# A four-layer graph network, last layer: each block's own columns on VectorE instead of through a diagonal matrix, and block 0's columns taken from on-chip memory

## The chip, the cores and the metric

The kernel runs on one core of one Trainium2 chip. The metric is the device time of one launch, in microseconds (us). The times before are three runs: 1054.39, 1056.62 and 1062.56 us, median 1056.62 us.

## The reference, cut to what matters

Four graph layers act on `x` (2708 nodes, 512 features) with a sparse weighted adjacency `adj` (2708 x 2708, every diagonal element non-zero). The change touches the last one only:

```python
bw  = sign(L3_gnn_weight)                  # 512 x 512
xw  = maximum(sign(x), 0) @ bw.T           # whole numbers, 2708 x 512
x   = layernorm(x + relu(adj @ xw))        # the last layer, and the output
```

`xw` holds whole numbers of at most 512 in size, so float16 holds them exactly. `adj` is float32.

## The kernel before, in words

The 2708 nodes are cut into 22 blocks of 128 rows (the last, block 21, has 20). Node 0 has the most neighbours and the density falls with the node's number, so the kernel treats the blocks in two ways:

- **Whole blocks**, 0 to 4 (`WHOLE3 = 5`): the product with all 2708 columns is formed densely, in 22 steps `j`, one for each block of source nodes. `whole_tile(j)` loads 128 rows of `xw` as float16 (`xs`), widens them to the 4-byte matmul type (`widened`), loads 128 x 640 elements of the transposed adjacency (`aw`), splits them into a high and a low half (`halves_of`: ScalarE copies the rounded value, VectorE subtracts it from the original), and runs 5 blocks x 2 halves = 10 matmuls of 128x128 by 128x512 (line L2001).
- **Sparse blocks**, 21 and then 5 to 20 (`order3`): for each block the nodes that any of its rows needs were listed earlier, in tiles of 128. `packed[b]` holds the matching columns of the adjacency, and GpSimd gathers the rows of `xw` by an indirect DMA per tile (`gathered`, line L584, tile `xg`; 76 gathers in this layer). Each tile costs two matmuls (L2040), one for each half. Blocks whose nodes nearly all are neighbours of block 0 take block 0's rows straight from `xw0`, which is on chip (`direct(b)`). GpSimd is used for the gathers alone in this layer.

A sparse block's own nodes are not in its list. Their only element is the diagonal `dia_own[:, b]`. Before, that product was a matmul too: the block's own `xw` rows are loaded (`xo`, L2013, two buffers) and widened (`wo`), ScalarE (L2021) and VectorE (L2024) build the high and the low half of a 128x128 diagonal matrix `dp`, and two matmuls (L2029) open the block's sum.

`finish3` closes a block: VectorE adds `relu(sum)` to the old features from PSUM (L1952), takes the statistics (L1954, L1956) and a few small steps for the inverse root, in pairs of blocks. ScalarE scales the row (L1969) and SyncE writes it out (L1973). The last block, 20, goes through this alone.

Two things set the order of the work. The loop over `order3` runs whole tiles between sparse blocks, a whole tile for each three gathers issued (`FETCHES3`), so that TensorE has work while gathers arrive. The tile scheduler then fixes a static order of instructions on each engine; every engine runs its own list in order. Buffers that matter: `parts` (high and low halves) has 4, `wide` (widened rows) 4, `aw` 4, `xs` 4, `xo` 2, gathered rows `xg` 11, PSUM sums of sparse blocks 3.

`packed[0]`, the transposed adjacency's columns of block 0 for all 22 source blocks, has been on chip since the first layer, but the whole blocks load these columns again as the first 128 of the 640.

Of the kernel before, what the change touches and what calls it, by code (L numbers as in the profile page):

```python
# [8 lines left out]
F32 = mybir.dt.float32  # L9
F32R = mybir.dt.float32r  # L10
# [3 lines left out]
AF = mybir.ActivationFunctionType  # L14
ALU = mybir.AluOpType
# [4 lines left out]
P = 128  # L20
# [27 lines left out]
WHOLE3 = 5  # L48
# [447 lines left out]
def sparse_layers(ctx, tc, x, adj, adj_t, w0_t, b0, w_sa, a_sa, w_gcnb, b_gcnb, wa, ba, wb, bb, w3_t,  # L496
# [11 lines left out]
    nc = tc.nc  # L508
    N, D = x.shape
    KC = D // P  # L510
    NB = -(-N // P)
# [1405 lines left out]
    with tc.tile_pool(name="s_l3", bufs=11, reuse_waits="tile") as lp, \  # L1917
# [1 line left out]
            tc.tile_pool(name="s_ps_3", bufs=3, reuse_waits="tile", space=PSUM) as ps_3:  # L1919
        W3 = WHOLE3 * P  # L1920
        CH3 = 4
        PW = max(CH3 * P, W3)

        def halves_of(a, r: int, w: int, name: str):

            p = lp.tile([P, 2, PW], F32R, tag="parts", name=f"p{name}", bufs=4)
            low, high = p[:r, 0, :w], p[:r, 1, :w]
            nc.scalar.copy(high, a)
            nc.vector.tensor_tensor(low, a, high.bitcast(F32), op=ALU.subtract)
            return p  # L1930
# [2 lines left out]

        def widened(t, r: int, name: str):

            g = lp.tile([P, D], F32R, tag="wide", name=f"w{name}", bufs=4)
            turn[0] += 1
            if turn[0] % 3 == 0:
                nc.vector.tensor_copy(g[:r], t[:r])
            else:  # L1940
                nc.scalar.copy(g[:r], t[:r])
            return g

        moments = []

        def finish3(b: int, ps, more: bool):

            m = rows(b)
            old = f[b] if b else first[1]
            k = len(moments)  # L1950
            t = old[:, :D]
            nc.vector.scalar_tensor_tensor(t[:m], ps[:m], 0.0, t[:m], op0=ALU.max, op1=ALU.add)  # L1952
            st = small.tile([P, 6], F32, tag="st", name=f"st_3_{b}")
            nc.vector.bn_stats(st[:m], t[:m])  # L1954
# [30 lines left out]

        whole = [ps_w.tile([P, D], F32, tag=f"w{b}", name=f"l3_{b}") for b in range(WHOLE3)]

        def whole_tile(j: int):
# [21 lines left out]
        for at, b in enumerate(order3):  # L2010
            m = rows(b)
            xo = lp.tile([P, D], F16, tag="xo", name=f"xo{b}", bufs=2)
            nc.sync.dma_start(xo[:m], xw_rows[b * P : b * P + m, :])  # L2013
            xo = widened(xo, m, f"o{b}")
            if at + 1 < len(order3) and at:
                gather3(order3[at + 1])
            src = [xw0] * len(direct(b)) + sources3.pop(b)
            ps = ps_3.tile([P, D], F32, tag="mm", name=f"l3_{b}")

            dp = lp.tile([P, 2, P], F32R, tag="dp", name=f"dp{b}", bufs=2)  # L2020
            nc.scalar.activation(  # L2021
                dp[:m, 1, :m], ident[:m, :m], AF.Copy, scale=dia_own[:m, b : b + 1]
            )
            nc.vector.scalar_tensor_tensor(  # L2024
                dp[:m, 0, :m], ident[:m, :m], dia_own[:m, b : b + 1],
                dp[:m, 1, :m].bitcast(F32), op0=ALU.mult, op1=ALU.subtract,
            )
            for h in range(2):
                nc.tensor.matmul(  # L2029
                    ps[:m], dp[:m, h, :m], xo[:m, :], start=(h == 0), stop=False  # L2030
                )
            for i0 in range(0, tiles(b), CH3):
                n = min(CH3, tiles(b) - i0)
                p = halves_of(
                    packed[b][:, i0 : i0 + n, :].rearrange("p n i -> p (n i)"), P, n * m,
                    f"{b}_{i0}",
                )
                for i in range(n):
                    for h in range(2):
                        nc.tensor.matmul(  # L2040
                            ps[:m], p[:, h, i * m : (i + 1) * m], src[i0 + i],
                            start=False, stop=(i0 + i == len(src) - 1 and h == 1),
                        )
# [88 lines left out]
```

## Time and profile before

| | |
|---|---|
| runs | 1054.39, 1056.62, 1062.56 us |
| profiled execution | 1000.5 us |
| its span, first to last instruction | 998.8 us |
| TensorE clock granted, mean | 0.968 |
| busy over the span | TensorE 88%, VectorE 66%, GpSimd 55%, ScalarE 39% |
| last layer: first product to last instruction | 881.0 to 998.8 us |

The page of the profile gives busy time by engine, the span in 40 slices, the DMA queues, the chain of work that ended last, and the costliest groups of instructions. A line such as "L1952 DVE SCALAR_TENSOR_TENSOR f<-l,f ... x21 | 14.4, 685 | 4.9 <-PE l L2040 4.8" says: line 1952, on VectorE, writes `f` from `l` and `f`, 21 times, 14.4 us busy, 685 ns each on average, 4.9 us idle of the engine just before these, 4.8 of it ended by a TensorE matmul of line 2040. PE is TensorE, PEld its weight loads, DVE VectorE, ACT ScalarE, POOL GpSimd, SP SyncE. Durations of instructions that run back to back overlap a little at their ends, so the spacing of their starts is the better price in a full queue. The profiled execution is 56 us shorter than the median of the runs; no view shows where the difference lies.

### The profile page before, as it was taken

What the parts mean: (1) busy time and instruction counts of PE and PEld (TensorE: products, weight loads), DVE (VectorE), ACT (ScalarE), POOL (GpSimd) and SP (SyncE); (2) the same over time, 40 slices, a digit from 0 to 9 for tenths busy, and PEclk for the clock granted to TensorE, in tenths of its full rate; (3) what the DMA queues carried; (4) which work ended last, traced back from release to release, by engine and by line L of the source; (5) the groups of instructions that cost most, each with busy time, mean ns of one, the idle gap of its engine ahead of it and who ended that gap; (6) DMA issues with size and microseconds to landing.
All of it is one profiled execution on the core that took longest, in us unless ns stands there. A gap on an engine that the chain in (4) does not pass through costs nothing.

```text
span 998.8 us, 13107 instructions
## 1 busy us (share of the span) xinstructions
PE 875.6 (88%) x3775; PEld 458.8 (46%) x3793; DVE 657.8 (66%) x2571; ACT 386.5 (39%) x821; POOL 549.6 (55%) x580
## 2 busy tenths in 40 slices
PE   1899997198999889999999989988989999789993
PEld 1555553022233244555555533444545555458872
DVE  4889998235677745555554356666768777647776
ACT  3667672000000125544444333333334333246564
POOL 1688888777777367645332154434343333057773
PEclk9999999599999999999999999999999999979998
DMA  9999984477778577766544476768487566289997
GB/s 275 351 360 363 359 273 118 131 217 230 243 248 256 157 223 217 225 186 207 190 138 126 138 265 242 249 225 273 156 264 231 191 200 209 86 248 340 356 262 230
DMA packets 96294, 231.16 MB, mean 231 GB/s; under 512 B 14204, under 2 KB 27884, under 8 KB 96212
## 3 DMA queue, kind: packets, MB, share of 16 engines
q0 software_dynamic: 46896, 139.22, 46.3%
q1 hardware_dynamic: 37368, 76.25, 22.2%
q10 hardware_dynamic: 11948, 14.76, 4.6%
q8 instruction: 32, 0.52, 0.2%
q14 instruction: 50, 0.41, 0.1%
HBM read 188.51 MB, written 31.71 MB: 220 GB/s over the span
## 4 chain that ended last, share of the span: by engine, by line
PE 53%; DMA 20%; DVE 16%; issue 4%; ACT 3%; POOL 3%; ACTq 0%; POOLq 0%; DVEq 0%; SPq 0%
PE l L1318 11%; DMA xg<-x_rows,i 10%; PE h L1535 8%; DMA xg<-y_rows,i 7%; PE l L2001 5%; PE a L1746 4%; PE e L1746 4%; PE l L2040 3%; PE y L1047 3%; PE pg L1798 2%; DVE s_mask L828 2%; PE pc L1798 2%; PE e L1568 2%; PE a L1569 2%; POOL xg L584 1%
## 5 line engine op out<-in xcount | busy, mean ns | idle before, releaser
L1723 POOL DMA_INDIRECT xg<-x_rows,i x107 | 105.3, 984 | 170.3 <-PE a L1746 39.9
L584 POOL DMA_INDIRECT xg<-x_rows,i x107 | 103.7, 969 | 95.8 <-PE l L1318 60.7
L1014 POOL DMA_INDIRECT a<-in_adj_t_dram,row_at x107 | 115.9, 1083 | 52.2 <-issue 24.9
L584 POOL DMA_INDIRECT xg<-y_rows,i x107 | 105.9, 989 | 32.6 <-issue 13.1
L1318 PE MATMUL l<-xg,a 128*64 128x512 f32 (+1 forms) x214 | 99.8, 628 | 27.2 <-DMA xg<-y_rows,i 26.5
L584 POOL DMA_INDIRECT xg<-xw_rows,i x76 | 79.0, 1039 | 31.2 <-issue 12.9
L1746 PE MATMUL a<-xg,a 128*64 128x512 f32 (+1 forms) x214 | 92.8, 603 | 3.3 <-DMA xg<-x_rows,i 3.3
L1746 PE MATMUL e<-xg,ae 128*64 128x512 f32 (+1 forms) x214 | 90.3, 603 | 3.1 <-ACT ae L1496 2.9
L1047 PE MATMUL y<-s_w,xt 128*128 128x512 f32 (+1 forms) x176 | 83.6, 620 | 0.0
L1535 PE MATMUL h<-s_wsa,xt 128*128 128x256 f32 (+3 forms) x352 | 82.0, 386 | 0.1
L1318 PE MATMUL l<-xg,inc 128*64 128x512 f32 (+1 forms) x214 | 78.0, 604 | 3.0 <-DMA xg<-x_rows,i 3.0
L1535 PEld LDWEIGHTS h<-s_wsa,xt 128*128 128x128 f32 (+1 forms) x352 | 63.9, 186 | 25.7 <-ACT xt L1530 9.9
L1491 ACT ACTIVATE ae<-sl,xg 128x64 f32<-128x64 f32 (+1 forms) x107 | 37.6, 360 | 98.4 <-DMA xg<-x_rows,i 90.4
L1318 PEld LDWEIGHTS l<-xg,a 128*64 128x64 f32 (+1 forms) x214 | 24.6, 153 | 81.3 <-DMA xg<-y_rows,i 61.0
L765 ACT ACTIVATE unused<-arow 128x1408 uint8<-128x1408 f32 (+3 forms) x44 | 58.4, 1326 | 3.2 <-DMA x_rows<-s_zero 2.4
L1426 DVE SCALAR_TENSOR_TENSOR t<-l,s_dinv,f 128x512 f32<-128x512 f32 (+1 forms) x21 | 15.7, 749 | 55.6 <-PE l L1318 55.6
L613 ACT ACTIVATE rsqs<-mv 128x1 f32<-128x1 f32 (+2 forms) x56 | 11.3, 202 | 100.3 <-DVE mv L642 95.6
L2001 PE MATMUL l<-ws,pw 128*128 128x512 f32 (+1 forms) x210 | 50.1, 392 | 0.0
L1492 DVE SCALAR_TENSOR_TENSOR ae<-ae 128x128 f32<-128x128 f32 (+5 forms) x56 | 19.3, 344 | 45.1 <-ACT ae L1491 44.8
L1047 PEld LDWEIGHTS y<-s_w,xt 128*128 128x128 f32 (+1 forms) x176 | 32.5, 195 | 34.5 <-issue 34.4
L1798 PE MATMUL pg<-s_wg,pt 128*128 128x256 f32 (+1 forms) x176 | 44.6, 391 | 3.0 <-ACT pt L1786 3.0
L638 DVE BATCH_NORM_STATS2 st<-t 128x6 f32<-128x512 f32 (+1 forms) x66 | 45.2, 685 | 0.2
(302 smaller groups left out, 1813.6 us busy)
## 6 DMA issues: line engine op xcount, KB each, us to landing
arow<-in_adj_dram SPq DMA_DIRECT2D x21, 704.0 KB
arow<-in_adj_dram SPq DMA_DIRECT2D x21, 650.0 KB
x_rows<-f SPq DMA_DIRECT2D x41, 256.0 KB
aw<-in_adj_t_dram SPq DMA_DIRECT2D x21, 320.0 KB
f<-in_x_dram SPq DMA_DIRECT2D x20, 256.0 KB
y_rows<-yt ACTq DMA_DIRECT2D x20, 256.0 KB
out_dram<-f SPq DMA_DIRECT2D x20, 256.0 KB
x_rows<-h SPq DMA_DIRECT2D x19, 257.0 KB
```

Of the source, the lines that this page charges most:

```text
L584: nc.gpsimd.indirect_dma_start(out=t, out_offset=None, in_=src[:, :], in_offset=bass.IndirectOffsetOnAxis(ap=index[b][:, i : i + 1], axis=0),)
L638: nc.vector.bn_stats(st[:m], t[:m])
L765: nc.scalar.activation(unused[:m, : ar.shape[1]], ar, AF.Copy, accum_out=row_sums[:m, b, h : h + 1])
L1014: nc.gpsimd.indirect_dma_start(out=packed[b][:, t + len(direct(b)), :], out_offset=None, in_=adj_t, in_offset=bass.IndirectOffsetOnAxis(ap ...
L1047: nc.tensor.matmul(ps[:m], xt[:, k, :m], w0[:, k, :], start=(k == 0), stop=(k == KC - 1))
L1318: nc.tensor.matmul(ps[r0:r1], weights, moving, start=(i == order[0]), stop=all(span(b, j) != (r0, r1) for j in order[order.index(i) + 1 :] ...
L1491: nc.scalar.activation(ev[:, i, :], sl, AF.Identity, bias=score)
L1535: nc.tensor.matmul(ps, xt[:, k, :m], w[:, k, :], start=(k == 0), stop=(k == KC - 1))
L1723: nc.gpsimd.indirect_dma_start(out=g, out_offset=None, in_=x2_rows[:, :], in_offset=bass.IndirectOffsetOnAxis(ap=index[b][:, t : t + 1], a ...
L1746: nc.tensor.matmul(ps[r0:r1], weights, moving, start=(i == order[0]), stop=all(span(b, k) != (r0, r1) for k in order[order.index(i) + 1 :] ...
L1798: nc.tensor.matmul(ps, pt[:, k, :m], w[:, k, :], start=(k == 0), stop=(k == KC - 1))
L2001: nc.tensor.matmul(whole[b], p[:r, h, b * P : (b + 1) * P], g[:r, :], start=(j == 0 and h == 0), stop=(j == NB - 1 and h == 1),)
```

## The change

1. Sparse blocks: the diagonal matrix, its two matmuls and the widening of the own rows go. `finish3` gets the float16 row `xo` and starts with one VectorE instruction, `u = xo * dia_own + sum` (float16 row from SBUF, sum from PSUM, float32 result in SBUF, one buffer). The relu-and-add then reads `u` instead of PSUM.
2. Whole blocks: `aw` is loaded without its first 128 columns (128 x 512 instead of 128 x 640), and block 0's weights come from `packed[0]`, split into halves for four steps `j` at a time (`parts0`, two buffers).
3. `wide` has 3 buffers instead of 4 and now serves the whole tiles only, so every third of these is widened on VectorE. `halves_of` takes its shape as (tiles, width).

```diff
-        PW = max(CH3 * P, W3)
-        def halves_of(a, r: int, w: int, name: str):
-            p = lp.tile([P, 2, PW], F32R, tag="parts", name=f"p{name}", bufs=4)
-            low, high = p[:r, 0, :w], p[:r, 1, :w]
+        PW = max(CH3 * P, W3 - P)
+        def halves_of(a, r: int, shape, name: str, tag: str = "parts", bufs: int = 4):
+            n, w = shape
+            p = lp.tile(
+                [P, 2, PW if tag == "parts" else CH3 * P], F32R, tag=tag, name=f"p{name}", bufs=bufs
+            )
+            p = p[:, :, : n * w].rearrange("p h (n i) -> p h n i", n=n)
+            low, high = p[:r, 0], p[:r, 1]
             nc.scalar.copy(high, a)
             nc.vector.tensor_tensor(low, a, high.bitcast(F32), op=ALU.subtract)
...
-            g = lp.tile([P, D], F32R, tag="wide", name=f"w{name}", bufs=4)
+            g = lp.tile([P, D], F32R, tag="wide", name=f"w{name}", bufs=3)
...
-        def finish3(b: int, ps, more: bool):
+        def finish3(b: int, ps, more: bool, own=None):
...
+            if own is not None:
+                u = lp.tile([P, D], F32, tag="u3", name=f"u3_{b}", bufs=1)
+                nc.vector.scalar_tensor_tensor(
+                    u[:m], own[:m], dia_own[:m, b : b + 1], ps[:m], op0=ALU.mult, op1=ALU.add
+                )
+                ps = u
             nc.vector.scalar_tensor_tensor(t[:m], ps[:m], 0.0, t[:m], op0=ALU.max, op1=ALU.add)
...
-            a = lp.tile([P, W3], F32, tag="aw", name=f"aw{j}", bufs=4)
-            nc.sync.dma_start(a[:r], adj_t[j * P : j * P + r, :W3])
-            p = halves_of(a[:r], r, W3, f"w{j}")
+            a = lp.tile([P, W3 - P], F32, tag="aw", name=f"aw{j}", bufs=4)
+            nc.sync.dma_start(a[:r], adj_t[j * P : j * P + r, P:W3])
+            p = halves_of(
+                a[:r].rearrange("p (n i) -> p n i", n=WHOLE3 - 1), r, (WHOLE3 - 1, P), f"w{j}"
+            )
+            if j % CH3 == 0 or j == NB - 1:
+                n = min(CH3, NB - 1 - j) if j < NB - 1 else 1
+                first_block[:] = j, halves_of(
+                    packed[0][:r, j : j + n, :], r, (n, P), f"z{j}", "parts0", 2
+                )
+            j0, p0 = first_block
             for b in range(WHOLE3):
                 for h in range(2):
+                    weights = p[:r, h, b - 1, :] if b else p0[:r, h, j - j0, :]
                     nc.tensor.matmul(
-                        whole[b], p[:r, h, b * P : (b + 1) * P], g[:r, :],
+                        whole[b], weights, g[:r, :],
...
             nc.sync.dma_start(xo[:m], xw_rows[b * P : b * P + m, :])
-            xo = widened(xo, m, f"o{b}")
...
-            dp = lp.tile([P, 2, P], F32R, tag="dp", name=f"dp{b}", bufs=2)
-            nc.scalar.activation(
-                dp[:m, 1, :m], ident[:m, :m], AF.Copy, scale=dia_own[:m, b : b + 1]
-            )
-            nc.vector.scalar_tensor_tensor(
-                dp[:m, 0, :m], ident[:m, :m], dia_own[:m, b : b + 1],
-                dp[:m, 1, :m].bitcast(F32), op0=ALU.mult, op1=ALU.subtract,
-            )
-            for h in range(2):
-                nc.tensor.matmul(
-                    ps[:m], dp[:m, h, :m], xo[:m, :], start=(h == 0), stop=False
-                )
...
-                            start=False, stop=(i0 + i == len(src) - 1 and h == 1),
+                            start=(i0 + i == 0 and h == 0),
+                            stop=(i0 + i == len(src) - 1 and h == 1),
...
-            finish3(b, ps, not pending and b not in (order3[0], order3[-1]))
+            finish3(b, ps, not pending and b not in (order3[0], order3[-1]), xo)
```

More of the change, by code (lines that the diff above doesn't have):

```diff
@@ L1986, in sparse_layers @@
         whole = [ps_w.tile([P, D], F32, tag=f"w{b}", name=f"l3_{b}") for b in range(WHOLE3)]
+        first_block = [0, None]
         def whole_tile(j: int):
@@ L2018, in sparse_layers @@
             ps = ps_3.tile([P, D], F32, tag="mm", name=f"l3_{b}")
-            dp = lp.tile([P, 2, P], F32R, tag="dp", name=f"dp{b}", bufs=2)
-            nc.scalar.activation(
-                dp[:m, 1, :m], ident[:m, :m], AF.Copy, scale=dia_own[:m, b : b + 1]
-            )
-            nc.vector.scalar_tensor_tensor(
-                dp[:m, 0, :m], ident[:m, :m], dia_own[:m, b : b + 1],
-                dp[:m, 1, :m].bitcast(F32), op0=ALU.mult, op1=ALU.subtract,
-            )
-            for h in range(2):
-                nc.tensor.matmul(
-                    ps[:m], dp[:m, h, :m], xo[:m, :], start=(h == 0), stop=False
-                )
             for i0 in range(0, tiles(b), CH3):
                 n = min(CH3, tiles(b) - i0)
[L2034 to L2037, printed above, removed]
+                p = halves_of(packed[b][:, i0 : i0 + n, :], P, (n, m), f"{b}_{i0}")
                 for i in range(n):
@@ L2040, in sparse_layers @@
                         nc.tensor.matmul(
-                            ps[:m], p[:, h, i * m : (i + 1) * m], src[i0 + i],
-                            start=False, stop=(i0 + i == len(src) - 1 and h == 1),
+                            ps[:m], p[:, h, i, :], src[i0 + i],
+                            start=(i0 + i == 0 and h == 0),
+                            stop=(i0 + i == len(src) - 1 and h == 1),
                         )
             pending = bool(moments)
-            finish3(b, ps, not pending and b not in (order3[0], order3[-1]))
+            finish3(b, ps, not pending and b not in (order3[0], order3[-1]), xo)
             if j == NB and whole and len(moments) == 1:
```

## The prediction

> **What bounds the kernel now.** The change touches the last layer only: the compiled order of instructions of both kernels differs on no engine before it. So I read the stage, not the page's totals. First the groups of instructions from 879 us on, for the prices; then the busy time by stretch, for who is full where; then the chain of waits from 955 us on, for what ends last; then the timeline of the last blocks.
>
> ```profile
> L584 POOL DMA_INDIRECT xg<-xw_rows,i x76 | 79.0, 1039 | 31.2 <-issue 12.9 <-DMA xw_rows<-xw 7.6 <-PE l L2040 6.8
> L1929 DVE TENSOR_TENSOR pw<-aw,pw 128x640 fp32r<-128x640 f32 (+1 forms) x22 | 18.1, 825 | 8.1 <-ACT pw L1928 7.8 <-DMA xs<-xw_rows 0.3
> L1952 DVE SCALAR_TENSOR_TENSOR f<-l,f 128x512 f32<-128x512 f32 (+1 forms) x21 | 14.4, 685 | 4.9 <-PE l L2040 4.8
> L2029 PE MATMUL l<-wo,dp 128*128 128x512 f32 (+1 forms) x34 | 11.2, 411 | 0.6 <-DVE dp L2024 0.6
> L2021 ACT ACTIVATE dp<-s_ident,s_dia_own 128x128 fp32r<-128x128 f32 (+1 forms) x17 | 6.6, 395 | 1.2 <-PE l L2029 0.8 <-ACT xw L1865 0.4
> L2024 DVE SCALAR_TENSOR_TENSOR dp<-s_ident,s_dia_own,dp 128x128 fp32r<-128x128 f32 (+1 forms) x17 | 5.7, 338 | 4.8 <-ACT dp L2021 4.6
> ```
> ```profile
> 881.00:895.00 14.00, 14.00 (x50) 11.19 (x50) 5.47 (x9) 5.64 (x11) 10.76 (x11) 0.80 1.12 335
> 895.00:958.00 63.00, 63.00 (x277) 51.47 (x277) 46.43 (x117) 39.86 (x77) 48.61 (x46) 1.00 1.16 329
> 958.00:992.00 34.00, 25.32 (x97) 18.50 (x96) 27.35 (x101) 18.87 (x39) 19.62 (x20) 0.95 0.98 286
> ```
> (columns: stretch, length, then busy us of PE, PEld, DVE, ACT, POOL, clock, DMA share, GB/s)
> ```profile
> 976.83 0.60 DVE p L1929
> 977.44 0.04 issue
> 977.48 2.77 PE l L2040 x8
> ...
> 983.71 0.69 DVE f L1952
> ...
> 985.81 0.58 DVE p L1929
> 986.40 0.04 issue
> 986.44 2.12 PE l L2040 x8
> ```
> ```profile
> 977.79 0.95 POOL L584 DMA_INDIRECT xg<-xw_rows,i  x1 [0.31 <-issue]
> ...
> 982.81 0.95 POOL L584 DMA_INDIRECT xg<-xw_rows,i  x1 [0.30 <-issue]
> 982.94 0.30 PEld L2040 LDWEIGHTS l<-xg,p 128*128 128x128 f32 x2 [0.36 <-DMA xg<-xw_rows,i]
> ```
>
> To be seen: up to 958 us TensorE has no idle time at all. But GpSimd is equally full in its own way: after the first gather (881.12) the next follows 0.30 us after the one before, to the last at 982.81, so 75 gathers take 101.7 us, 1.36 us each. TensorE cannot change that stream. After 964 us the chain is VectorE, and at 982.94 TensorE waits for a gather itself.
>
> **What the Trainium skill says.** "SBUF — State Buffer", section "Who interferes with whom": a VectorE instruction with two SBUF inputs contends with GpSimd's SBUF reads; it infers that making descriptors is spared. Here it is not: the gather of 886.47 us took 1.59 us instead of 0.95, under a low half (L1929, two SBUF inputs) from 886.42 to 887.25; nearly all long gathers begin under such a one. The measurement decides. "VectorE: DVE Perf Modes", "Why PSUM operands drop a tier": with a PSUM operand a float32 instruction runs at the plain rate; L1952 (one input PSUM, one SBUF, 512 elements) shows 685 ns. "DMA: Bandwidth & Descriptors", "Anatomy of one DMA — SWDGE (gpsimd) path": about 2 us fixed per such DMA; here the gather issued at 977.79 was usable at 982.94, 5.2 us later, on queues 98% busy.
>
> **The change part by part.**
>
> *TensorE.* 34 matmuls go (17 blocks x 2). Their spacing in the full queue is 0.2265 us (20 of L2001 in the chain take 4.53), so 34 x 0.2265 = 7.7 us; 12 pairs of these (blocks 21, 5 to 15) lie before 966 us: 5.4 us. The order of the others is unchanged.
>
> *ScalarE.* Gone: 17 x 0.395 = 6.7 (dp), 10 x 0.613 = 6.1 (own rows). Whole rows 16 to 14: 1.2. High halves 640 to 512 wide: 22 x (0.728 - 0.619) = 2.4. Added: five block-0 groups at 0.619 and one of 0.29: 3.4. Net 13.0 less. ScalarE is on the chain for little; worth nothing alone.
>
> *VectorE.* Gone: 17 x 0.338 = 5.7 (dp), 7 x 0.43 = 3.0 (own rows), 22 x (0.825 - 0.686) = 3.1 (narrower low halves). Added: whole rows 5 to 7, 0.9; block-0 groups 5 x 0.686 + 0.29 = 3.7; the own-column add `u`, 17 x 0.685 = 11.6. The trace of before has no float16 row with a PSUM sum; nearest are L1952, 0.685, and L1836 with two float32 rows from SBUF, 0.752. I take 0.685, as the one whose input is PSUM too; the other end adds 1.1 in all. Below 0.6 (the spacing of these in the chain) nothing speaks for it. Net +4.4 us. In 895 to 958 VectorE is 74% busy; the change adds about 0.3 us per block there, hidden by its idle quarter.
>
> *GpSimd and DMA.* The 76 gathers stay. Low halves in all take 34 us before and after (3.1 less, 3.7 more), so the lengthening of gathers stays (76 x (1.039 - 0.95) = 6.8 us); the new add has one SBUF input only. `aw` shrinks by 64 KB each, 1.4 MB of 37.3 MB from 860 us on, about 5 us of DMA time at the 269 GB/s of that stretch. That may shorten landings a little: 0 to 1 us.
>
> *The start.* Before, the last `xw` copy on ScalarE (877.87) is followed by two dp (0.5 us together) and the first high half; the first low half ends at 880.95. Now two block-0 groups stand first on both engines, about 0.5 each more, 0.1 back from the narrower half: block 1's first low half ends about 881.4. Block 0's two matmuls can run before, so the ten that began at 880.99 lose nothing: 0, between -0.3 and +0.5.
>
> *Rows `xo`.* They are freed by `u` instead of by the widening, so the fetch for block b+2 waits for `u` of block b. On SP, block 18's and 19's fetch now stands behind the output of blocks 13 and 14, and block 20's behind those of 15 and 0, which wait for ScalarE. From `u` of 16 to `u` of 18 there are eleven 0.6 us instructions, about 8 us; from 17 to 19 about 6. The slowest fetch in the tail took 4.83 us (958.24 to 963.08). Covered; if not, what is short is at most 2 us, once or twice. The wait that went, ScalarE's for that fetch (1.6 us at 963), gives nothing, since gathers follow.
>
> *The middle.* TensorE gets ahead by 5.4 us at block 15: its gathered tiles would be used at 966.24 - 5.4 = 960.8. The DMA packet records put the last packet of block 15's last gather at 961.2 and, for blocks 16 to 20, at 965.5, 970.2, 975.8, 981.8 and 986.1; gather 72 was usable 1.1 us after its last packet. So from block 15 on TensorE meets the gathers, and the 5.4 us are gone. VectorE likewise starts its backlog earlier and then waits for blocks.
>
> *The end.* Block 19's sum is complete at 983.7 as before. Before, VectorE then ran: f (0.60), two small, two statistics (1.20), one small, block 20's low half, done 986.40. In the compiled order now: `u` of 19, two small, f of 19, two small, its statistics, four small, f of block 4, one small, then block 20's low half: five of 0.60 and nine small of 0.07, 3.7 us: 987.4. That is +1.0. Block 20's last gather, usable at 987.2, covers only part of it, since eight matmuls take 2.1 us from there: 989.5 instead of 988.55. Then `u` of 20 stands alone in the last chain: +0.70. The rest (statistics, root, scale, output) is the same.
>
> Sum: 0 + 0 + 1.0 + 0.7 = **+1.7 us**, on the profiled execution 1000.5 to 1002.2. The median of the runs is 56 us more than the profiled execution; I carry +1.7 over: 1056.6 + 1.7 = 1058.3 us.
>
> **The rivals.**
>
> *TensorE's time reaches the end.* In the runs something is 56 us slower than in the profile. If that is TensorE, it needs longer than the gathers up to 987 us, and what is removed counts: -7.7 + 0.7 = -7.0, 1049.6 us. For it: TensorE 88% busy, no gap up to 958. Against: the profiled stage meets the gathers, and only 1 us lies between block 20's last gather and its last matmul. Chance 0.20.
>
> *VectorE's queue becomes the bound (slower).* Each `u` waits at the head of an in-order queue for its block's last matmul, with low halves for the next tiles behind it; TensorE waits for these. It decides as soon as TensorE has no prepared tile left, and then each of blocks 5 to 20 costs 16 x 0.685 = 11.0 us: 1067.6. For it: TensorE already waited 2.3 us twice for a low half (977.48, 986.44). Against: before, f stood in that queue with the same wait, and TensorE did not stop before 965. Chance 0.16, half of it with less than the full price.
>
> *The row fetch is late.* As above, 2 us twice: 1056.6 + 1.7 + 4 = 1062.3. Chance 0.04.
>
> **How the numbers follow.** Gathers and the VectorE end 0.60, the others as given. The first case alone spans about -2 (landings earlier) to +5 us (a dearer add, a small bunching on VectorE), 1054.6 to 1061.6, before the runs' own spread of 8 us. I reach down to the TensorE case and up into half of the VectorE case: 1049 to 1066. About 1% (10.6 us) is what a measurement of this kernel can tell from no change; faster than that needs more than all matmuls removed: 0.05. Slower than that is half of the VectorE case: 0.08. Within: 0.87.
>
> **What would show it.** Right: no L2029 group, 17 adds of about 0.69 us, the gathers still 1.36 us apart with the last about 983, TensorE idle for gathers from block 15 on, block 20's low half about 987.4, the end about 1000.5 in the span. Wrong: a last gather well before 982 or after 985; adds of over 0.8 us; TensorE idle before 950; `u` waiting for `xo`; or runs that gain 7 us although the profile does not.

## The result, and the profile after

Before: 1064.26 us median of 22 runs (1054.39 to 1074.41). After: 1061.72 us median of 22 runs (1055.08 to 1075.1). The ratio is 0.9998, 95% interval 0.9976 to 1.002: -0.2 us, give or take 2.3. (The ratio is worked out from the fast runs alone and is not that of the two medians, 0.9976, which lies at the edge of the interval.) The change makes no difference here that can be measured; the forecast was +1.7 us. The median of the three runs that the forecast started from, 1056.62 us, is 7.6 us below that of all 22.

One thing has to be said ahead of all numbers: executions came in two kinds whatever the kernel, about 1000 us long or 1055 us and more, and the profile that the prediction used (1000.5 us) is of the first kind, while these runs are of the second. In the second kind the 76 gathers are still 0.30 us apart for the most part, but some stand 1.5 to 2.2 us apart, and the other engines rest there too (at the first pause shown below, VectorE and ScalarE start again at 943.68 us and GpSimd at 944.10). Below, "with pauses" means these. Each ratio is against runs of the kernel before beside it on the same chip, which were of the same kind; profiles are compared within a kind. A difference between two such ratios, given below in us, joins the intervals of both. The profile after, with pauses, groups of the last stage:

```profile
L584 POOL DMA_INDIRECT xg<-xw_rows,i x76 | 77.6, 1021 | 39.9 <-issue 17.8 <-DMA xw_rows<-xw 7.6 <-PE l L2022 5.7
L1933 DVE TENSOR_TENSOR pw<-aw,pw 128x512 fp32r<-128x512 f32 (+1 forms) x22 | 15.1, 691 | 12.9 <-issue 8.7 <-ACT pw L1932 4.2
L1958 DVE SCALAR_TENSOR_TENSOR u<-xo,s_dia_own,l 128x512 f32<-128x512 f16 (+1 forms) x17 | 12.5, 738 | 3.0 <-issue 1.7 <-PE l L2045 1.4
L1962 DVE SCALAR_TENSOR_TENSOR f<-u,f 128x512 f32<-128x512 f32 (+1 forms) x17 | 11.6, 681 | 0.0
```

The 34 matmuls of line 2029 and the `dp` rows are gone. The 17 adds are there at 738 ns (I took 685). Next come the same stage by stretch (columns: stretch, length, busy us of PE, PEld, DVE, ACT, POOL, clock, DMA share, GB/s), two of GpSimd's gathers that follow a pause (the idle time before each is in brackets), and the end of the chain of waits:

```profile
928.00:942.00 14.00, 14.00 (x55) 11.21 (x55) 4.91 (x9) 5.15 (x10) 10.63 (x11) 0.87 1.15 334
942.00:1005.00 63.00, 56.70 (x241) 44.27 (x240) 42.60 (x102) 29.67 (x58) 42.30 (x42) 1.00 1.04 294
1005.00:1055.00 50.00, 29.44 (x95) 19.34 (x93) 34.99 (x119) 18.27 (x36) 24.64 (x23) 0.76 0.77 227
```
```profile
944.10 0.95 POOL L584 DMA_INDIRECT xg<-xw_rows,i  x1 [2.24 <-PE l L2045]
...
954.41 0.95 POOL L584 DMA_INDIRECT xg<-xw_rows,i  x1 [1.45 <-PE l L2022]
```
```profile
1039.15 0.57 DVE f L1962
1039.79 0.61 DVE p L1933
1040.45 3.79 PE l L2045 x8
1044.27 0.76 DVE u L1958
1045.05 0.70 DVE f L1962
```

Two readings. In the middle TensorE is busy 56.7 of 63 us, where before, in the other kind of execution, it had no hole. And the chain ends as forecast, with block 20's low half (`p`), eight matmuls, then `u` alone; but the eight matmuls take 3.79 us, where before's took 2.12.

To compare like with like, the kernel before was profiled again with pauses (x1). Last stage, in us from the start of the first gather:

| | before | before again (x1) | after | after again (x12) |
|---|---|---|---|---|
| pauses | no | yes | yes | no |
| last gather starts | 101.7 | 109.2 | 109.0 | 102.4 |
| last matmul ends | 107.4 | 118.7 | 116.2 | 109.6 |
| last scaling on ScalarE ends | 111.4 | 122.7 | 120.9 | 114.4 |
| end | 117.6 | 128.3 | 126.5 | 119.9 |
| wait ahead of block 20's last eight matmuls | 2.31 | 3.65 | 3.78 | 3.78 |
| these eight take | 2.11 | 3.50 | 3.78 | 3.78 |

So the last stage reads as 1.8 us shorter in the profiles with pauses and as 2.3 us longer in those without. These are single profiles, and the two with pauses differ in their pauses too: beyond the usual 0.30 us the gathers' holes come to 6.8 us in x1 and 9.4 us in the profile after. Their traces also hold little more than half of the semaphore updates (9734 in the profile after, 17500 in that of x12), so that what is named there as the end of a wait is less sure.

### The profile page after: what moved, and what is told of

The parts are those of the page before. It is cut to its first block, busy times and chain, and to the rows that moved or that the text cites. A ratio compares the mean times of both kernels' runs of the same rounds, so it can differ in the third digit from the quotient of the medians.

```text
span 1054.6 us, 13041 instructions
## 1 busy us (share of the span) xinstructions
PE 893.0 (85%) x3759; PEld 459.7 (44%) x3759; DVE 658.8 (62%) x2573; ACT 373.9 (35%) x799; POOL 548.8 (52%) x580
## 4 chain that ended last, share of the span: by engine, by line
PE 55%; DVE 14%; DMA 12%; issue 8%; ACT 5%; another core or an unknown queue 3%; POOL 3%; ACTq 0%; POOLq 0%; SPq 0%; DVEq 0%
PE l L1318 14%; DMA xg<-x_rows,i 8%; PE h L1535 7%; PE e L1746 4%; PE a L1746 4%; PE l L2022 4%; PE y L1047 3%; PE l L2045 2%; PE pg L1798 2%; PE pc L1798 2%; DMA xg<-y_rows,i 2%; PE l L1373 2%; PE e L1568 2%; PE a L1569 1%
## 5 line engine op out<-in xcount | busy, mean ns | idle before, releaser
L1014 POOL DMA_INDIRECT a<-in_adj_t_dram,row_at x107 | 114.9, 1073 | 67.1 <-issue 24.9
L1318 PE MATMUL l<-xg,a 128*64 128x512 f32 (+1 forms) x214 | 96.5, 661 | 4.4 <-issue 2.7
L1047 PE MATMUL y<-s_w,xt 128*128 128x512 f32 (+1 forms) x176 | 93.2, 679 | 0.0
L1047 PEld LDWEIGHTS y<-s_w,xt 128*128 128x128 f32 (+1 forms) x176 | 35.9, 216 | 40.8 <-issue 40.7
L2045 PE MATMUL l<-xg,p 128*128 128x512 f32 (+1 forms) x152 | 44.3, 434 | 10.3 <-DVE p L1933 6.2
L1542 DVE COPY h<-h 128x260 f32<-128x260 f32 (+1 forms) x20 | 8.6, 428 | 62.8 <-PE h L1535 47.6
L2022 PE MATMUL l<-ws,pw 128*128 128x512 f32 (+1 forms) x168 | 42.3, 394 | 4.9 <-issue 4.5
```

Source lines behind the costliest of these rows:

```text
L1014: nc.gpsimd.indirect_dma_start(out=packed[b][:, t + len(direct(b)), :], out_offset=None, in_=adj_t, in_offset=bass.IndirectOffsetOnAxis(ap ...
L1047: nc.tensor.matmul(ps[:m], xt[:, k, :m], w0[:, k, :], start=(k == 0), stop=(k == KC - 1))
L1318: nc.tensor.matmul(ps[r0:r1], weights, moving, start=(i == order[0]), stop=all(span(b, j) != (r0, r1) for j in order[order.index(i) + 1 :] ...
L2022: nc.tensor.matmul(whole[b], weights, g[:r, :], start=(j == 0 and h == 0), stop=(j == NB - 1 and h == 1),)
L2045: nc.tensor.matmul(ps[:m], p[:, h, i, :], src[i0 + i], start=(i0 + i == 0 and h == 0), stop=(i0 + i == len(src) - 1 and h == 1),)
```

## The experiments

**What the 56 us are: before once more.** The unchanged kernel.

> The kernel before, unchanged, as a second profile of it. The first profile of before (998.8 us span, TensorE clock 0.968) is shorter than every one of its 22 runs; the profile after (1054.6 us, clock 0.942) is like the runs. Both theories expect a ratio of 1.000 within the spread of the runs. If the 56 us between the two profiles are a matter of the execution and not of the change, this profile shows a span of 1050 to 1070 us, with about 120 us of idle time put down to issue on POOL and some 50 to 80 on VectorE and ScalarE, as the profile after has and the first one of before has not. If they come from the change, it shows about 1000 us again.

Ratio 1.0006 (0.9982 to 1.0031), span 1057.2 us. The 56 us belong to the execution and not to the change. GpSimd's holes come to 6.8 us beyond 0.30 us each in this stage, against 0.6 in the first profile. What makes the pauses was not found.

**VectorE's adds left out, with and without pauses (x2, x13).**

`finish3` no longer gets the row, so that it leaves the add out and reads the sum from PSUM:

```diff
-            finish3(b, ps, not pending and b not in (order3[0], order3[-1]), xo)
+            finish3(b, ps, not pending and b not in (order3[0], order3[-1]))
```

> The changed kernel without the own-column add u: the diagonal product of the sparse blocks is left out altogether. Theory A (gathers set the pace from block 15 on; only the end of VectorE's queue costs): about 2 us faster than the changed kernel, so a ratio of 0.997 to 1.000 to before. Rival B (the removed TensorE time did reach the end, and VectorE's add of 11.6 us took it back): 7 to 12 us faster, a ratio of 0.989 to 0.993.

> The changed kernel without the 17 adds of the own product (left out of the sum). Theory L: 1 to 3 us faster than x12: 0.7 for the last chain, 1.0 or less for block 20's low half, and up to 1.7 if TensorE is not slowed in its last eight matmuls. Rival N (VectorE's row of 11.6 us more is what the changed kernel ends by): 6 us or more faster than x12.

x2: 1.002 (0.9997 to 1.0044). x13: 1.0025 (1.0008 to 1.0042), that is 1.1 us less than x12 (the changed kernel without pauses, below), give or take 2.4. So the 17 adds do not cost the 6 or 7 us of rivals B and N; theory L's 1 to 3 us can't be told from nothing. In x13's profile ScalarE does end earlier (111.6 us after the first gather instead of 114.4), but the kernel doesn't (120.1 and 119.9). ScalarE's and SyncE's lines of time at the end of x13:

```profile
987.37 0.20 ACT L613 ACTIVATE rsqs<-mv 128x1 f32<-128x1 f32 x1 [0.79 <-DVE mv L1973]
987.48 3.62 ACT L1979 ACTIVATE f<-f,rs 128x512 f32<-128x512 f32 x5
```
```profile
988.30 4.10 SPq L1983 DMA_DIRECT2D out_dram<-f  x5
```

Block 20 has caught up with four blocks ahead of it: five scalings run back to back, five outputs of 256 KB are issued within 4.1 us, and the program ends 8.5 us after the last scaling, against 5.6 in x12. In these two profiles the earlier end of the sums is paid back behind the scalings; no run tried the output queue by itself.

**TensorE's low products left out, with and without pauses (x3, x15).**

```diff
-                for h in range(2):
+                for h in (1,):
...
-                        start=(j == 0 and h == 0), stop=(j == NB - 1 and h == 1),
+                        start=(j == 0), stop=(j == NB - 1),
```

> The changed kernel with the whole blocks' products of the low halves left out: 110 of the 220 matmuls of the whole tiles go, 25 us of TensorE at 0.2265 us each, while the low halves are still computed. Theory A: the gathers set the end, TensorE's time is hidden; 0 to 3 us faster than before, a ratio of 0.997 to 1.000. Rival B (TensorE sets the time of the last layer): 20 us or more faster, a ratio of 0.98.

> The changed kernel with the low products of the whole blocks left out, 110 matmuls less, 24.9 us of TensorE. Theory L: within 2 us of x12, since the gathers set the time. Rival M: 7 us or more faster than x12.

x3: 1.001 (0.9985 to 1.0036). x15: 1.0075 (1.0048 to 1.0103, seven runs), 3.9 us *slower* than x12, give or take 3.3; theory L had said within 2. Taking 25 us from TensorE gains nothing in either kind, so the prediction's first rival is dead. The slowing has its place in the groups of x12 (first) and x15 (second):

```profile
L584 POOL DMA_INDIRECT xg<-xw_rows,i x76 | 80.4, 1057 | 30.6 <-issue 12.9 <-DMA xw_rows<-xw 7.6 <-PE l L2045 6.1
```
```profile
L584 POOL DMA_INDIRECT xg<-xw_rows,i x76 | 84.2, 1108 | 30.6 <-issue 11.1 <-DMA xw_rows<-xw 7.6 <-PE l L2045 5.8
```

The gathers took 3.8 us longer and their idle time is the same. Why they were lengthened here was not tried apart; profiles without pauses had means from 1010 to 1108 ns.

**16 gathers left out (x4), the same with the next block's halves prepared ahead (x10).**

```diff
         def gather3(b: int):
+            if 17 <= b <= 20:
+                sources3[b] = [xw0] * ROOM[b]
+                return
```

> The changed kernel with the 16 gathers of blocks 17 to 20 left out (their matmuls read block 0's rows, which are on chip): GpSimd's stream is 16 x 1.36 = 22 us shorter, all other work is the same. Theory A: the end moves forward until TensorE's and VectorE's own work ends; TensorE is 5 us ahead and VectorE's queue has its idle quarter, so 5 to 12 us faster, a ratio of 0.988 to 0.995. Rival B (TensorE or VectorE is the bound): within 2 us, a ratio of 0.998 to 1.002.

> The gathers of blocks 17 to 20 left out (these blocks read block 0's rows in their place) and, from block 15 on, the halves of the next block prepared ahead of the adds, max and statistics of this one. 16 fewer gathers alone gained 4.8 us, and the move alone nothing. Theory G: with the gathers out of the way TensorE's last wait is for block 20's low half on VectorE (5.99 us in that profile), and the move takes it away: -7 to -9 us in all. Rival I (VectorE's whole row, not the place of that one instruction, is next): -5 us as without the move.

x4 (pauses): 0.9955 (0.993 to 0.9979), -4.8 us of 22, just short of theory A's 5 to 12. x10 (no pauses): 0.9966 (0.9946 to 0.9985), -3.4 against before and so 7.0 less than x12, give or take 2.6. By time alone that leaves both theory G (-7 to -9) and rival I (-5); the trace decides. x10 by stretch and TensorE's line of time:

```profile
976.00:988.00 12.00, 3.78 (x8) 2.48 (x8) 11.93 (x45) 5.97 (x12) 0.00 (x0) 0.72 0.44 156
```
```profile
981.82 3.78 PE L2056 MATMUL l<-xw,p 128*128 128x512 f32 x8 [6.20 <-DVE p L1933]
```

Theory G had the move take TensorE's last wait for a low half away. It did not: 5.99 us in x4, 6.20 here. VectorE is busy 11.93 of these 12 us, as rival I has it. With the gathers out of the way VectorE is next in line, a few us behind them. Leaving gathers out takes time from GpSimd and load from the DMA queues alike; no run tells the two apart.

**Each half of the change alone (x5, x6).** x5 is the kernel before with block 0's columns from `packed[0]`; x6 the changed kernel with these loaded again:

```diff
-            a = lp.tile([P, W3 - P], F32, tag="aw", name=f"aw{j}", bufs=4)
-            nc.sync.dma_start(a[:r], adj_t[j * P : j * P + r, P:W3])
+            a = lp.tile([P, W3], F32, tag="aw", name=f"aw{j}", bufs=4)
+            nc.sync.dma_start(a[:r], adj_t[j * P : j * P + r, :W3])
...
-                    weights = p[:r, h, b - 1, :] if b else p0[:r, h, j - j0, :]
+                    weights = p[:r, h, b, :]
```

> The kernel before with the second half of the change alone: the whole blocks take block 0's columns from memory on chip (five groups of 4 and one of 1, their own ring of 2), the column transfers shrink to 512, the diagonal matrices and their 34 matmuls stay. Theory A (the stage ends by two chains that close within 2 us of each other, the 76 gathers and VectorE's row of block sums; neither contains this part): 0, between -2 and +2 us. Rival C (the change hides two effects that cancel: this part slows the start of the stage and VectorE, and the other part gains it back): +3 us or more here, and -3 or less for the other part.

> The first half of the change alone: own columns added on VectorE from the float16 row, no diagonal matrix; the column transfers and the low halves stay 640 wide. Theory A: 0, between -2 and +2 us. Rival C (two effects that cancel): -3 us or less here.

0.9998 (0.9967 to 1.0029) and 0.9994 (0.9969 to 1.0019), both with pauses: neither half differs from before. Two cancelling effects of the 3 us that rival C asked for lie at or beyond the edges of these intervals; smaller ones aren't excluded, and without pauses the halves weren't run apart.

**The add three times (x7).**

```diff
+                for again in range(2):
+                    v = lp.tile([P, D], F32, tag="v3", name=f"v3_{b}_{again}", bufs=1)
+                    nc.vector.scalar_tensor_tensor(
+                        v[:m], own[:m], dia_own[:m, b : b + 1], ps[:m], op0=ALU.mult, op1=ALU.add
+                    )
```

> The changed kernel with the own-column add of every block done three times (two into a buffer that nobody reads): 34 instructions more on VectorE, 34 x 0.70 = 23.8 us. Theory A: the idle quarter of VectorE takes those of blocks 5 to 14; from block 15 on VectorE's row is one of the two closing chains, so some 6 blocks x 1.4 = 8 us and 1.4 in the last chain come through, less what the gathers cover: +4 to +9 us. Rival D (VectorE has a free quarter to the end, gathers alone set the time): +1.4 us, the last block's two adds alone. Rival E (VectorE is the bound of the whole stage): +20 us or more.

1.0134 (1.0084 to 1.0184, six runs): +14.4 us (9.0 to 19.7), more than theory A's 4 to 9, less than rival E's 20, and far from rival D's 1.4. VectorE's busy time in the stage rose from 82.2 (after) to 102.8 us, by 20.6; so some 6 us of it were hidden, with an interval of about 1 to 12. By stretch, its last 63 us:

```profile
1017.00:1080.00 63.00, 33.18 (x117) 24.59 (x115) 49.26 (x141) 19.94 (x39) 25.55 (x26) 0.75 0.65 191
```

VectorE is the fullest there, 78%; TensorE and GpSimd are about half empty. The longest wait of the changed kernel's TensorE for a low half was 3.78 us; here two took 5.09 and 9.65. So the VectorE rival names a real edge. The change's net +4.4 us on VectorE (an estimate of the prediction) seems to stop short of it.

**Block 20's halves ahead (x8, x14).**

```diff
+            halves = made.pop(b, None) or halves3(b)
...
-                p = halves_of(packed[b][:, i0 : i0 + n, :], P, (n, m), f"{b}_{i0}")
+                p = next(halves)
...
+            if b != NB - 1 and 15 <= b < NB - 2:
+                made[b + 1] = iter(list(halves3(b + 1)))
             pending = bool(moments)
```

> The changed kernel with one move in the order: from block 15 on, the halves of the next block are prepared ahead of the adds, max and statistics of this one, so block 20's low half no longer stands behind those of block 19 and block 4 on VectorE. Nothing is added or removed. Theory A: TensorE then waits for the gathers alone at the end; block 20's low half was done at 1040.4 in the profile of the changed kernel and its eight matmuls took 3.79 us from there instead of 2.1, because the last gather landed about 1.7 us later, so 0 to -2 us. Rival F (the place of block 20's low half in VectorE's order sets the end): -3 us or more. If the move puts the sums of 16 to 19 later and these set the end: slower by 1 to 2 us.

> The changed kernel with the halves of the next block prepared ahead of the adds, max and statistics of this one from block 15 on. Theory L: 0.5 to 2.5 us faster than x12, since block 20's low half no longer makes TensorE wait. If VectorE's whole row is what ends last there: the same as x12.

1.0002 (0.9975 to 1.003) with pauses, 1.0037 (1.0019 to 1.0055) without: the same as the changed kernel in its kind. TensorE's weight loads for the sparse blocks waited for low halves and for gathers as follows, x12 (first) and x14 (second):

```profile
PEld l L2045 <- DVE p L1933: 4.7, 2, 4.5
PEld l L2045 <- DMA xg<-xw_rows,i: 4.5, 7, 1.1
```
```profile
PEld l L2053 <- DVE p L1933: 0.4, 1, 0.4
PEld l L2053 <- DMA xg<-xw_rows,i: 7.7, 11, 1.5
```

(engine, tile and line, what it waited for: us in all, times, longest.) The wait for the low half turns into waits for gathers, and no gain can be seen from moving that one low half in VectorE's order, the +1.0 of my sum: rival F falls, and theory L's 0.5 to 2.5 us for x14 did not come. What I expected of x8 also gave a late gather as the reason for the 3.79 us of the last eight matmuls; the clock, below, explains them better.

**16 gathers more (x9).** One more per block, into a buffer that nobody reads.

```diff
             sources3[b] = [gathered(lp, D, xw_rows, b, t, F32R) for t in range(ROOM[b])]
+            if 5 <= b <= 20:
+                z = lp.tile([P, D], F32R, tag="xz", name=f"xz{b}", bufs=1)
+                nc.gpsimd.indirect_dma_start(
+                    out=z, out_offset=None, in_=xw_rows[:, :],
+                    in_offset=bass.IndirectOffsetOnAxis(ap=index[b][:, 0:1], axis=0),
+                )
```

> The changed kernel with one gather more for each of blocks 5 to 20, into a buffer of its own that nobody reads: 16 more on GpSimd, 16 x (1.02 + 0.30) = 21 us of its stream. Theory G (GpSimd's stream, VectorE's row and TensorE's row are of nearly one length, tied by the 4 buffers of halves and the 11 of gathered rows; VectorE has about 9 us to spare, 23.8 less the 14.4 that came through with the add done thrice; the gathers have none, since 16 fewer gained 4.8 us and no more): +17 to +21 us. Rival H (the gathers too are held up by the others, GpSimd's waits for TensorE and its pauses take part of it): +10 us or less.

1.037 (1.0337 to 1.0403), without pauses: +37.2 us, more than either. The table of waits has a wait that I had added:

```profile
POOL xz L1992 <- DMA xz<-xw_rows,i: 17.9, 6, 3.5
```

With one buffer, an extra gather waits for the landing of the one before. 21 us of gathers and 17.9 of waits are 39 us put into GpSimd's stream, and 37.2 - 3.6 (x12) = 33.6 came out; the last gather starts at 136.5 instead of 102.4 us, 34.1 later. So most of what is put into this stream reaches the end, and rival H falls. The waits, which I had not meant to add, keep this from being a measure of 16 gathers, and the extra rows load the DMA queues as well.

**High products twice (x11).**

```diff
-                    nc.tensor.matmul(
-                        whole[b], weights, g[:r, :],
-                        start=(j == 0 and h == 0), stop=(j == NB - 1 and h == 1),
-                    )
+                    for again in range(1 + h):
+                        nc.tensor.matmul(
+                            whole[b], weights, g[:r, :],
+                            start=(j == 0 and h == 0),
+                            stop=(j == NB - 1 and h == 1 and again == 1),
+                        )
```

> The changed kernel with the high product of every tile of the whole blocks done twice: 110 matmuls more on TensorE, 110 x 0.2265 = 24.9 us (the sum of the whole blocks is therefore another one). Left out, 110 such matmuls gained nothing. Theory G: TensorE's row has room for the 7.7 us that the diagonal matrices took in the kernel before, and in the profile of the changed kernel it is busy 99.9 of 116.2 us, so about 8 to 14 us are absorbed: +11 to +17 us. Rival J (TensorE is already one of the bounds, the 7.7 us were lost elsewhere): +22 us or more. Rival K (TensorE is nowhere near): +5 us or less.

1.0246 (1.0215 to 1.0278, six runs), without pauses: +24.7 against before, 24.7 - 3.6 = 21.1 against x12 for 24.9 us of matmuls. So the changed kernel's TensorE has about 4 us to spare, with an uncertainty of 4. Theory G's 8 to 14 is too much. The number is near rival J's, its reason is not: if TensorE were the bound, x15 would have gained. Less TensorE time gives nothing, more is paid for almost at once. GpSimd's waits for TensorE, x12 (first) and x11 (second), show how it is paid:

```profile
POOL xg L584 <- PE l L2045: 6.1, 20, 0.3
```
```profile
POOL xg L584 <- PE l L2047: 26.1, 24, 5.1
```

A gather needs a free one of the 11 buffers of rows, and TensorE frees them. With TensorE late, gathers wait for it for up to 5.1 us, and the last one starts at 121.7 instead of 102.4 us. "TensorE cannot change that stream", as the prediction has it, holds for less work on TensorE, and not for more.

**The change itself without pauses (x12).** The changed kernel as it is.

> The changed kernel as it is. Theory L (the sum of the prediction holds in an execution without the pauses, plus the last eight matmuls at half the granted clock, 3.78 instead of 2.11 us, which the sum did not have): +1.7 to +3.5 us. Rival M (TensorE's 7.7 us count there, since its row is without a gap up to 958 us in that profile): -3 to -7 us. In an execution with the pauses: 0, as before.

1.0036 (1.0019 to 1.0054): +3.6 us (1.9 to 5.4). Theory L gave 1.7 to 3.5; rival M's gain falls. TensorE's line of time:

```profile
974.74 0.73 PE L2045 MATMUL l<-xg,p 128*128 128x512 f32 x2 [0.51 <-DMA xg<-xw_rows,i]
976.17 0.73 PE L2045 MATMUL l<-xg,p 128*128 128x512 f32 x2 [0.70 <-DMA xg<-xw_rows,i]
978.16 1.19 PE L2045 MATMUL l<-xg,p 128*128 128x512 f32 x2 [1.26 <-DMA xg<-xw_rows,i]
980.61 3.80 PE L2045 MATMUL l<-xg,p 128*128 128x512 f32 x8 [1.26 <-DMA xg<-xw_rows,i]
...
993.57 3.78 PE L2045 MATMUL l<-xg,p 128*128 128x512 f32 x8 [3.78 <-DVE p L1933]
```

From 974.7 us, block 17, TensorE waits for one gather after the other: what the removed matmuls gave is spent there, as forecast. By stretch, x12 (first) and before (second) at block 20:

```profile
988.00:990.00 2.00, 1.78 (x4) 0.50 (x2) 0.17 (x1) 0.30 (x1) 1.55 (x2) 0.50 1.01 291
990.00:993.40 3.40, 0.00 (x0) 0.00 (x0) 3.40 (x13) 1.45 (x3) 0.95 (x1) 0.50 1.03 295
993.40:995.50 2.10, 1.93 (x5) 1.55 (x6) 1.79 (x12) 1.12 (x4) 0.00 (x0) 0.50 0.67 250
```
```profile
984.00:986.40 2.40, 0.13 (x1) 0.00 (x0) 2.40 (x9) 1.61 (x3) 0.00 (x0) 1.00 0.84 236
986.40:988.60 2.20, 2.11 (x8) 1.43 (x8) 1.65 (x15) 1.32 (x3) 0.00 (x0) 1.00 0.58 210
```

The column of the clock (the last but two) reads 0.50 against 1.00: the same eight matmuls take 3.78 us instead of 2.11. It reads 0.50 from 988 us on, before the wait of 3.78 us has begun: the clock was already down after the short waits for gathers, and the long one only kept it there.

The lines of x12 show one more thing, a gather that begins under the relu-and-add of the changed kernel (line 1962), and below it one that begins under that of the kernel before (line 1952):

```profile
906.29 0.67 DVE L1962 SCALAR_TENSOR_TENSOR f<-u,f 128x512 f32<-128x512 f32 x1
906.37 1.42 POOL L584 DMA_INDIRECT xg<-xw_rows,i  x1 [0.30 <-issue]
```
```profile
964.21 0.69 DVE L1952 SCALAR_TENSOR_TENSOR f<-l,f 128x512 f32<-128x512 f32 x1
964.49 0.95 POOL L584 DMA_INDIRECT xg<-xw_rows,i  x1 [0.30 <-issue]
```

Line 1952 read the sum from PSUM; line 1962 reads `u`, and so has two inputs in SBUF. The seven gathers of x12 that begin under it took 1.19 to 1.45 us, the five that begin under the add `u` itself 0.94 to 0.95, and ten of before's eleven that begin under line 1952 0.95. In x13, where line 1962 reads PSUM again, all gathers together take 77.3 us instead of 80.4 (before: 79.0), and the last one starts at 99.3 instead of 102.4. The prediction counted the inputs of `u` and not those of the instruction behind it. What this is worth at the end isn't known, since x13 gains no more than 1.1 us.

**Filling the holes (x16, x17, x18).** Matmuls whose result is thrown away, ahead of block 20's (x16), of the last five blocks' (x17), and of these with the halves ahead (x18).

```diff
             ps = ps_3.tile([P, D], F32, tag="mm", name=f"l3_{b}")
+            for _ in range({20: 12}.get(b, 0)):
+                nc.tensor.matmul(ps[:m], xw0[:, :m], xw0, start=True, stop=True)
```

> The changed kernel with 12 matmuls that nobody reads (into block 20's own sum, which its first real matmul starts anew) ahead of block 20's. They stand in the 3.78 us in which TensorE waits for block 20's low half. Theory P (the clock is halved because TensorE has stood idle): the last eight matmuls take 2.1 to 2.9 us instead of 3.78, and the kernel is 0.9 to 1.7 us faster than the changed one (+2 to +3 us against before in an execution without pauses). Rival Q (the clock at the end does not depend on the hole): 3.78 as before, no gain, and up to 1 us lost if the twelve, at half the clock, take 5.5 us and outlast the hole.

> The changed kernel with such matmuls ahead of the last five blocks' (4, 4, 6, 6 and 12 of them for blocks 16 to 20), 32 x 0.2265 = 7.2 us, about what the diagonal matrices had taken. Theory P: clock 1.0 over the whole end, the last eight in 2.1 us, 1.5 to 3 us faster than the changed kernel. Rival Q: the same as the changed kernel or up to 2 us slower.

> The changed kernel with the halves of the next block ahead of this one's adds, max and statistics from block 15 on, and with 4, 4, 6, 6 and 6 matmuls that nobody reads ahead of blocks 16 to 20. Theory P: the move alone gained nothing because what it gave went to the halved clock; with the clock kept, 2 to 4 us faster than the changed kernel, which is even with before in an execution without pauses. Rival Q: the same as the changed kernel.

All three ran with pauses: 0.9992 (0.9964 to 1.0019), 1.0003 (0.9981 to 1.0026), 0.9987 (0.9964 to 1.0009). TensorE's lines of time, x16 and then x17:

```profile
1053.28 4.07 PE L2041 MATMUL l<-xw 128*128 128x512 f32 x12
1057.27 2.12 PE L2047 MATMUL l<-xg,p 128*128 128x512 f32 x8
```
```profile
1048.79 2.90 PE L2041 MATMUL l<-xw 128*128 128x512 f32 x12
1055.08 3.40 PE L2047 MATMUL l<-xg,p 128*128 128x512 f32 x8 [3.38 <-DVE p L1933]
```

In x16 the twelve fill the hole. They begin at half the clock, take 4.07 us, and the last eight behind them run at the full clock, 2.12 us. In x17 the twelve run at the full clock (2.90 us) and are done 3.38 us too early; the hole is there again, and the eight take 3.40 us. So idle time before the eight brings the slow clock, and work before them lifts it, as theory P has it. That filling the hole makes the kernel faster is not shown: in x16 the last matmul ended at 116.5 us against 116.2 after, and the 1 to 3 us that theory P asked for in x16 and x17 are within the intervals of these runs, which came with pauses. x18, the candidate for a better version, is not told apart from no change either; its last eight took 4.02 us with waits for gathers between them.

## Why the prediction came out as it did

The prediction said "within 1%" with 0.87, and both kinds of execution are within it. That says little for the sum behind it: the range, 1049 to 1066 us, took in the TensorE case of -7 us as well as half of the VectorE case. The sum itself, +1.7 us, did not come out: the runs that it was carried to gave -0.2, give or take 2.3 (which just reaches +1.7, so that what failed there is read from the profiles), and without pauses, where it should have held, it was short.

- *Start, gathers, TensorE hidden.* Held. Both profiles have TensorE full in the first 14 us. Without pauses the last gather starts at 102.4 us instead of 101.7. The removed matmuls turn into waits for gathers (4.7 us of TensorE's in x12), and removing 110 more gains nothing (x3, x15). The holes begin at block 17, not 15.
- *Block 20's low half, +1.0.* In x12 it is done 105.8 us after the first gather, before at 105.3: +0.5.
- *The add in the last chain, +0.70.* It measured +0.78 (0.76 and the step of 0.02 to the next).
- *The step that failed without pauses: "eight matmuls take 2.1 us from there".* They took 3.78 us, +1.67, at half the clock. I had forecast that TensorE would stand idle for gathers, and priced its last eight matmuls as if that cost nothing. The 2.12 us came from a line of before that followed a wait of 2.31 us; the other line that I showed, at 977.48, follows a wait of 2.34 us, and its eight took 2.77. In that profile the clock is 0.78 from 977 to 980 us and 0.65 from 980 to 983. The sign was there, and I passed it over.
- *The sum with this term.* 0.5 + 1.67 + 0.78 = 2.95 us. ScalarE's last scaling is 3.0 us later in x12, the output takes 0.7 less in the profile, and the runs say +3.6 (1.9 to 5.4). This is the arithmetic of one chain in two profiles. Taking single terms out of it gained nothing that can be told from zero (x13, x14), so another chain probably lies close behind.
- *The step that failed for the runs: "I carry +1.7 over".* I took the sum from an execution without pauses to a median 56 us above it. With pauses, before already waits 3.65 us for block 20's low half and already pays 3.50 us for the eight matmuls, so two of the three terms are next to no difference there. Its TensorE also runs further behind the gathers (last matmul 9.5 us after the last gather's start, against 5.7 without pauses), which after the change is 7.2. That the two sides then cancel rests on one profile each and stays open; the ratio of 0.9998 alone is firm.
- *The rivals.* "TensorE's time reaches the end" falls in both kinds (x3, x15). "VectorE's queue" falls at its size of 11 us, but x7 and x10 show its edge a few us away. "The row fetch is late": in x12 the adds waited for the last matmul 9.8 us and for no `xo`, as the group's last columns show:

```profile
L1958 DVE SCALAR_TENSOR_TENSOR u<-xo,s_dia_own,l 128x512 f32<-128x512 f16 (+1 forms) x17 | 12.6, 741 | 10.7 <-PE l L2045 9.8 <-DMA aw<-in_adj_t_dram 0.8
```

Where the gain went, as far as the profiles without pauses show: the gathers cover it until block 20, and then it is given back, as a slower TensorE and a longer last chain, and, where that chain is shortened (x13), behind the bunched scalings.

## What to carry to other kernels

Where three engines' rows are within a few per cent of one length, ask what each is worth in both directions: here 25 us less of TensorE gave nothing, while 25 us more cost 21. Work taken from TensorE, which then waits for transfers, came back as a lower clock for what it still had to do (3.78 us instead of 2.11). When an operand moves from PSUM to SBUF, ask of every instruction that reads it what else now runs beside it. And before a sum from one profile is carried to a median, look whether the profile is of the same kind of execution: if its span is far off the runs, price the terms in both.

## What the runs showed of the hardware

- The clock at a hole. The Trainium skill, "TensorE: Matmul & The Clock Gate", "Part 1: The HAM clock gate", says that after at least one idle window of about 3.4 us the array runs at half its clock until it has been busy about as long. The profiles agree at the end of the stage: after waits of 3.38 us or more (ten profiles) the last eight matmuls took 3.40 to 3.79 us, and after the fillers of x16, 4.07 us long, 2.12. But shorter holes did it too, so here 3.4 us is no limit below which a wait is safe: in x12 the eight at 980.61 took 3.80 after four waits of 0.51 to 1.26 us within 7 us, and of two waits of nearly one length in before, 2.34 and 2.31 us, the first was followed by eight in 2.77 us and the second by eight in 2.11.
- Gathers under a VectorE instruction with two inputs in SBUF are longer. In x12 those that began under line 1962 (`u` and `f`, both in SBUF) took 1.19 to 1.45 us; before, ten of the eleven that began under line 1952 (the sum in PSUM, `f` in SBUF) took 0.95 us, and the eleventh, 2.24 us, ran on under a low half.
- The add with a float16 row from SBUF and a sum from PSUM took 738 to 741 ns for 512 elements. The same instruction took 681 ns on two float32 operands in SBUF (line 1962) and 685 ns with one of them in PSUM (before, line 1952).
- The pauses: in executions with them the gathers have five to nine holes of over 0.6 us, most of 1 to 2.5 us. Beyond the usual 0.30 they come to 6.8 us in x1, 9.4 in the changed kernel and 12.2 in x17; before has 0.6 us without pauses and x12 none. Their cause stays open.
